# A message-passing kernel on one core: the general path moves from the else-side of a branch to a branch of its own

## The chip, the core and the metric

The kernel runs on one core of one Trainium2 chip. The core has a matrix engine (PE, with its weight loads shown as PEld), a vector engine (DVE), an activation engine (ACT), a general engine (POOL) and a queue engine (SP) that issues transfers. Each of them has its own stream of instructions, takes its own branches, and meets the others only through semaphores: an instruction may wait until a semaphore has reached a number, and may add to one when it is done. The metric is the device time of one execution in microseconds; smaller is better. Times of before and after are medians of several runs.

## What is computed

The reference takes 1250 nodes with 512 features each and 40000 edges sorted by their target, and makes one block of an equivariant network (PaiNN), adds its input, and normalizes each row:

```python
x_j = x[src]
s_j = silu(x_j[:, 384:] @ W1 + b1) @ W3 + b3
edge_basis = rbf * cutoff @ W2 + b2
s1, s2, s3 = split(s_j * edge_basis)
v_msg = v_j * s1[:, :, None] + s3[:, :, None] * edge_attr1[:, None, :]
x = x + segment_sum(concatenate([v_msg, s2]), dst)      # first sum over edges
...
msg = update(x[src])                                     # U, V, Wu1, Wu2
x = x + segment_sum(msg, dst)                            # second sum over edges
return layernorm(x_in + x)
```

## The kernel before

A front part loads nodes, edges and weights, turns the node features into a table of 640 numbers per node in memory (`table1`, L584), and counts how many chunks of 512 edges have a target outside of the window of nodes that the fast path keeps for them (`missed_i`, L290). L383 loads that count into a register on every engine, and L384 branches on it: with a count of zero the engines run `windowed` (L587), otherwise `general` (L528), which is good for any order of edges. With the inputs of the reference the count is zero, so `general` is in the program but never runs. Before the change it is the else-side of the same branch (L386).

`windowed` goes over 79 steps. A step is four tiles of 128 edges (512 edges, of four chunks). In the order of the code (L1490 to L1503) step t does this:

- DVE makes the messages of the step (`messages`, L860): `hot` (L812) compares the edges' targets with the lanes, then L865, `pair` (L883), `spread` (L823) and L869 multiply the gathered rows with the edge factors `eb`. All of it reads `eb`, which has one buffer, and `hot` is the first that waits for it.
- PE adds up the messages of the step before (`add_messages`, L893: L900 four matmuls, L907 twelve), counts links (`count_links`, L914: L925 four), and then makes the next step's factors (`edge_factors`, L850: L854 four matmuls). These last cannot start before DVE's L869 has read the old factors. PE has some work besides in most steps (node updates), and from step 32 on it also begins the large second product (`begin_out`, L1257; `products`, L1245: the matmuls of L1248).
- POOL issues the four gathers for three steps later (`gather`, L739; L745), the first of them behind PE's `edge_factors`.
- ACT prepares one-hot tiles (L835, L845) and copies.

The program's extra work repeats every eight steps, so steps that lie eight apart do the same things. The next step's `hot` waits for PE's L854, and L854 waits for DVE's L869: this circle sets the pace. After the steps come the rest of the second product, the normalization and the output (`end_out` L1276, `norm_out` L1289, stores at L1303).

The build handles semaphores as follows. Each engine has one counting semaphore, and a waiting instruction waits for a number of it. The build takes an increment away where nobody waits for its number and adds it to a later increment of the same engine. Numbers run through the whole program. With the two paths as two sides of one branch, both start from the same number and must end at the same number; the shorter side gets its missing counts from one large increment at its start. Read out of the built program: PE stands at 42 when the branch comes; `windowed` counts from 42 to 2446; `general` starts with one increment of 1076 and counts from 1118 to 2446. On DVE it is `windowed` that starts with a large increment (1618), and on ACT too (324). Transfer semaphores are filled up in the same way: SP has eight semaphore instructions and POOL eight instructions (INC_SWDGE_SEM, reported under L1873) in `windowed` that do nothing else. An increment stays when a waiting instruction of either path names its number. So PE's matmuls of `windowed` mostly lose their increments below 1118 and mostly keep them above:

| matmuls of PE with an increment, built program before | steps 1 to 37 | steps 38 to 66 | steps 67 to 70 | steps 71 to 75 |
|---|---|---|---|---|
| of how many in a step | 24 to 32 | 26 to 34 | 31 to 34 | 26 to 34 |
| that increment | 1 to 4 | 18 in step 38, then 26 to 34 | 13 to 17 | 20 to 34 |

Of the kernel before, what the change touches and what calls it, by code (L numbers as in the profile page):

```python
# [64 lines left out]
def gnn_resnorm(  # L65
# [315 lines left out]
    front_scope.close()  # L381

    misses_v = nc.values_load(missed_i[0:1, 0:1], min_val=0, max_val=n_edges)  # L383
    with tc.If(misses_v == 0) as in_windows:  # L384
        windowed(tc, sh)
    with in_windows.Else():  # L386
        general(tc, sh)


# [1138 lines left out]
def general(tc, sh):  # L1528

    with ExitStack() as ctx:
        _general(ctx, tc, sh)
# [338 lines left out]
```

## Time and profile before

| | |
|---|---|
| median of 3 runs (lowest to highest) | 594.64 us (591.26 to 596.64) |
| the profiled execution's own time | 585.79 us |
| its span, first to last instruction | 583.8 us |
| mean granted clock of PE | 0.888 |
| busy PE / DVE / ACT / POOL | 445.5 / 441.8 / 373.6 / 354.5 us |
| all 16 transfer engines, mean over the span | 217 GB/s |
| the branch L384: PE, ACT, SP, DVE take it at | 25.7, 28.0, 28.7, 30.7 us |
| first and last `hot` (L812) | 41.0 and 537.7 us |
| end of `windowed`: SP leaves it at | 579.4 us |

A row of the timeline has start, duration, engine, line, operation, output and inputs, and in brackets how long the engine was idle before it and what ended that. A row of the windows view has the stretch, its length, each engine's busy time with its number of instructions, PE's granted clock, the transfer engines' busy share and GB/s. A row of the view of one source line has the queue, the operation, its number, shortest/median/longest duration in ns, and the first and last start. A 32-bit matmul leaves two rows in the trace, so a group of four matmuls reads "x8" and the twelve of L907 read "x24".

### The profile page before, as it was taken

The page shows a single profiled execution, that of the slowest core. Times are in us where ns is not written, and L with a number is a line of the kernel's source. Part 1 is how long each engine was busy: PE and PEld are TensorE (multiplying, and loading weights), DVE is VectorE, ACT ScalarE, POOL GpSimd, SP SyncE. Part 2 cuts the span into 40 slices and gives each one's busy share as a digit, 9 for nine tenths or more (in the row PEclk, how much of TensorE's full clock was granted, in tenths as well). Part 3 has the DMA queues.
Part 4 walks back from the last instruction along what each step waited for, and adds up shares of the span by engine and source line. Part 5 has one row for each costly group of instructions (what it writes and reads, how often), then busy time and mean ns, then how long its engine had stood idle before and what let it go on. Part 6 is the DMA issues. An engine that isn't in the chain of part 4 may idle for free. (4 is left out here: it accounts for less than half of the span.)

```text
span 583.8 us, 11028 instructions
## 1 busy us (share of the span) xinstructions
PE 445.5 (76%) x4193; PEld 240.2 (41%) x4193; DVE 441.8 (76%) x698; ACT 373.6 (64%) x941; POOL 354.5 (61%) x369
## 2 busy tenths in 40 slices
PE   2845667687777887697888786787777878798894
PEld 1422323344444344334435443443443444353673
DVE  7685867878878777878877777777787777687685
ACT  1455364757677665767776767777667778656455
POOL 7265767656667665656656665666666576643850
PEclk9966986888899777979888889998989899889998
DMA  8766777786777767767877777777777787859514
GB/s 240 257 189 213 200 224 216 210 262 200 216 224 243 228 197 218 214 205 220 253 245 201 253 226 213 233 231 242 220 229 224 218 240 224 241 148 285 210 38 146
DMA packets 38321, 126.95 MB, mean 217 GB/s; under 512 B 6688, under 2 KB 8238, under 8 KB 38258
## 3 DMA queue, kind: packets, MB, share of 16 engines
q0 software_dynamic: 26016, 104.86, 60.5%
q1 hardware_dynamic: 10910, 20.64, 10.2%
q10 hardware_dynamic: 1332, 0.64, 0.4%
q8 instruction: 35, 0.57, 0.4%
q14 instruction: 28, 0.23, 0.1%
HBM read 114.78 MB, written 11.34 MB: 216 GB/s over the span
## 5 line engine op out<-in xcount | busy, mean ns | idle before, releaser
L745 POOL DMA_INDIRECT more<-table,src_i x189 | 189.9, 1005 | 107.3 <-issue 44.0
L745 POOL DMA_INDIRECT nodes<-table,src_i x124 | 126.3, 1019 | 74.0 <-issue 28.3
L854 PE MATMUL eb<-w_sb,basis_t 25*128 25x388 f32 x626 | 83.5, 585 | 76.6 <-issue 42.2
L845 ACT ACTIVATE one<-one,weight,src_f 128x128 f16<-128x128 f16 x313 | 128.5, 482 | 0.5 <-issue 0.2
L835 ACT ACTIVATE one<-number,low 128x128 f16<-128x128 f16 x313 | 99.8, 392 | 8.5 <-PE adj L925 3.3
L812 DVE TENSOR_TENSOR hot<-lane,eb 128x128 f32<-128x128 f32 (+1 forms) x81 | 22.7, 281 | 81.6 <-PE eb L854 44.7
L869 DVE TENSOR_TENSOR more<-more,eb 128x1536 f32<-128x1536 f32 (+2 forms) x49 | 82.6, 1688 | 0.0
L854 PEld LDWEIGHTS eb<-w_sb,basis_t 25*128 25x128 f32 x626 | 27.5, 196 | 99.5 <-issue 58.0
L900 PE MATMUL agg<-more,hot 128*32 128x512 f32 (+1 forms) x378 | 66.0, 752 | 1.2 <-ACT sums L956 1.2
L865 DVE TENSOR_TENSOR more<-more,eb 128x1024 f32<-128x1024 f32 (+2 forms) x49 | 57.5, 1175 | 0.4 <-issue 0.3
L907 PEld LDWEIGHTS agg<-more,spread 128*32 128x32 f32 x1134 | 39.5, 125 | 40.8 <-issue 40.1
L869 DVE TENSOR_TENSOR nodes<-nodes,eb 128x1536 f32<-128x1536 f32 (+1 forms) x32 | 54.2, 1695 | 0.0
L907 PE MATMUL agg<-more,spread 128*32 128x128 f32 x1134 | 47.8, 298 | 0.0
L823 DVE TENSOR_TENSOR spread<-hot,eb 128x384 f32<-128x384 f32 (+1 forms) x81 | 43.0, 532 | 0.0
L925 PE MATMUL adj<-pair,one 128*128 128x160 f16 x313 | 37.9, 243 | 5.0 <-issue 4.9
L900 PE MATMUL agg<-nodes,hot 128*32 128x512 f32 x248 | 38.5, 680 | 2.4 <-ACT sums L956 2.4
L883 DVE TENSOR_TENSOR pair<-number,column 128x640 f16<-128x640 f16 (+1 forms) x81 | 38.5, 476 | 0.0
L805 ACT COPY basis_t<-work 128x512 f32<-128x512 f32 x20 | 11.7, 587 | 41.1 <-PE work L800 21.7
L865 DVE TENSOR_TENSOR nodes<-nodes,eb 128x1024 f32<-128x1024 f32 (+1 forms) x32 | 37.8, 1180 | 0.0
L960 DVE SCALAR_TENSOR_TENSOR both<-both,adj 128x400 f16<-128x400 f16 (+1 forms) x20 | 11.3, 566 | 32.0 <-ACT both L951 21.1
L907 PEld LDWEIGHTS agg<-nodes,spread 128*32 128x32 f32 x744 | 23.6, 116 | 23.1 <-issue 22.9
L925 PEld LDWEIGHTS <-one 128*128 128x128 f16 x313 | 20.8, 100 | 22.1 <-issue 20.7
(258 smaller groups left out, 728.8 us busy)
## 6 DMA issues: line engine op xcount, KB each, us to landing
table<-more SPq DMA_DIRECT2D x10, 320.0 KB
spilled<-begun SPq DMA_DIRECT2D x12, 256.0 KB
more<-table,src_i POOLq DMA_INDIRECT x189
more<-spilled SPq DMA_DIRECT2D x2, 1280.0 KB
resid<-h_t SPq DMA_DIRECT2D x9, 256.0 KB
node_x<-in_x_dram SPq DMA_DIRECT2D x8, 256.0 KB
nodes<-table,src_i POOLq DMA_INDIRECT x124
nodes<-in_x_dram POOLq DMA_DIRECT2D x2, 768.0 KB
```

Source lines behind the costliest of these rows:

```text
L745: got = nc.gpsimd.indirect_dma_start(out=rows_t[:n, j, :], out_offset=None, in_=sh.table1, in_offset=bass.IndirectOffsetOnAxis(ap=sh.src_i ...
L812: nc.vector.tensor_tensor(hots[t][:m, js, :], lane[:m, None, :WIN].to_broadcast(shape), eb[:m, js, V + 3 : V + 4].to_broadcast(shape), op= ...
L823: nc.vector.tensor_mul(spread[t][:m, js], hots[t][:m, js, None, :].to_broadcast(shape), eb[:m, js, V : V + 3, None].to_broadcast(shape),)
L835: nc.scalar.activation(onehots[t][:, j, :], number[:, :P], AF.Abs, bias=low[:, e : e + 1])
L845: nc.scalar.activation(one, one, AF.Relu, scale=less[:, e : e + 1], bias=worth[:, e : e + 1])
L854: made = nc.tensor.matmul(eb[:, j, : V + CARRY], turned[g][rows, i, :], sh.w2_sb[rows, :], start=True, stop=True,)
L865: nc.vector.tensor_mul(msg[:m, js, V:], msg[:m, js, V:], eb[:m, js, C:V])
L869: nc.vector.tensor_mul(msg[:m, js, :V].rearrange("p t (k c) -> p t k c", k=3), msg[:m, js, :V].rearrange("p t (k c) -> p t k c", k=3), eb[ ...
L883: nc.vector.tensor_tensor(pair[:m, js, :].rearrange("p t (l h) -> p t l h", h=2), number[:m, : PARTS * WIN].rearrange("p (l h) -> p l h", ...
L900: nc.tensor.matmul(agg[j * WIN : (j + 1) * WIN, :], hots[t][:m, j, :], msg[:m, j, :width], start=(i == 0), stop=False, skip_group_check=True,)
L907: nc.tensor.matmul(agg[j * WIN : (j + 1) * WIN, c * C : (c + 1) * C], spread[t][:m, j, c, :], msg[:m, j, width:], start=False, stop=(i == ...
L925: nc.tensor.matmul(to[:, :, at : at + WIN], one[:m, j, :], pair[:m, j, :].rearrange("e (p n) -> e p n", n=WIN), start=(i == 0 and j == js[ ...
```

## The change

The condition is tested twice instead of once. `general` gets a branch of its own, behind the one of `windowed`, with the opposite condition on the same register:

```diff
     misses_v = nc.values_load(missed_i[0:1, 0:1], min_val=0, max_val=n_edges)
-    with tc.If(misses_v == 0) as in_windows:
+    with tc.If(misses_v == 0):
         windowed(tc, sh)
-    with in_windows.Else():
+    with tc.If(misses_v != 0):
         general(tc, sh)
```

No line of `windowed`, and no line of what comes before it, differs. What the build makes of it differs. The two paths now follow each other in the program and in the semaphores' numbers: PE counts in `windowed` from 42 to 2446 and in `general` from 2446 on; DVE's and ACT's large increments at the start of `windowed` are gone. The order of the engines' instructions in `windowed` is the same, except for these:

| in `windowed` of the built program | before | after |
|---|---|---|
| PE matmuls with an increment, of 2404 | 1359 | 276 |
| of these in a step, steps 38 to 75 | 13 to 34 | 2 to 5 |
| DVE instructions with an increment, of 646 | 636 | 363 |
| ACT, of 903 | 827 | 772 |
| SP's semaphore instructions that fill up a count | 8 | 0 |
| POOL's INC_SWDGE_SEM | 8 | 0 |

The number for which an instruction waits stands for the same releasing instruction as before. Each branch without an else gets a small block that fills up the counts when the branch is not taken: eight semaphore instructions and a jump on SP, a semaphore instruction, four waits, one INC_SWDGE_SEM and a jump on POOL, a semaphore instruction and a jump on each of the others. With these inputs every engine leaves `windowed` by a jump over the first such block, tests the condition again (L386), jumps over `general` to the second such block, runs it, and goes on to the end of the program. Before, it jumped over `general` straight to the end. In SP's stream the first of the two jumps goes over 9 instructions, the jump over `general` over some 430.

## The prediction

> **What bounds the kernel now.** I read the page first, then the timeline around single steps, then windows cut at the starts of steps, and the rows of the branch and of the end last. No engine is full:
>
> ```profile
> span 583.8 us, 11028 instructions
> PE 445.5 (76%) x4193; PEld 240.2 (41%) x4193; DVE 441.8 (76%) x698; ACT 373.6 (64%) x941; POOL 354.5 (61%) x369
> ```
>
> PE and DVE are both busy for 76% and wait for each other in each of the 79 steps: DVE's `hot` (L812) needs PE's factors (L854), and L854 needs DVE's L869. The row of L812 shows where these steps lie, 496.7 us from the first `hot` to the last:
>
> ```profile
> L812 DVE TENSOR_TENSOR hot<-lane,eb x81: 172/286/289, 41.0 to 537.7; 128x128 f32<-128x128 f32 x76, 128x64 f32<-128x64 f32 x4, 64x32 f32<-64x32 f32 x1
> ```
>  So the pace of a step decides, and of it the hole between DVE's L869 and the next `hot`.
>
> The built program offers a comparison inside this one trace. Up to step 37 a step's matmuls carry 1 to 4 semaphore increments; from step 38 to 66 nearly every one of the 26 to 34 carries one. The change makes the second kind of step into the first. So I cut two stretches of 32 steps each, steps 7 to 38 and 39 to 70, each four rounds of the eight-step pattern, and two single rounds out of the first:
>
> ```profile
> 87.60:287.30 199.70, 155.54 (x1593) 82.52 (x1586) 155.76 (x225) 132.89 (x340) 129.92 (x128) 0.85 0.74 222
> 287.30:492.10 204.80, 165.69 (x1692) 87.70 (x1695) 156.71 (x228) 147.53 (x370) 129.09 (x128) 0.93 0.76 229
> ...
> 185.80:237.60 51.80, 40.92 (x410) 22.26 (x402) 39.22 (x57) 34.98 (x89) 32.18 (x32) 0.80 0.71 213
> 237.60:287.30 49.70, 38.84 (x403) 19.86 (x396) 39.45 (x58) 33.77 (x88) 32.52 (x32) 0.86 0.75 224
> ```
>
> The first column after the stretch is its length. The stretch with many increments takes 204.80 us against 199.70, that is 6.40 against 6.24 us a step, although PE's granted clock was higher in it (0.93 against 0.85). DVE's busy time is the same (156.71 and 155.76): the difference is waiting.
>
> Now the hole itself, in steps of equal place in the pattern. The first four pairs have few increments, the last four many; each pair is L869 and the next step's `hot`:
>
> ```profile
> 103.36 1.75 DVE L869 TENSOR_TENSOR nodes<-nodes,eb 128x1536 f32<-128x1536 f32 x1
> ...
> 106.17 0.29 DVE L812 TENSOR_TENSOR hot<-lane,eb 128x128 f32<-128x128 f32 x1 [0.29 <-PE eb L854]
> ...
> 201.72 1.74 DVE L869 TENSOR_TENSOR more<-more,eb 128x1536 f32<-128x1536 f32 x1
> ...
> 204.63 0.28 DVE L812 TENSOR_TENSOR hot<-lane,eb 128x128 f32<-128x128 f32 x1
> ...
> 233.75 1.75 DVE L869 TENSOR_TENSOR more<-more,eb 128x1536 f32<-128x1536 f32 x1
> ...
> 237.61 0.29 DVE L812 TENSOR_TENSOR hot<-lane,eb 128x128 f32<-128x128 f32 x1 [1.71 <-PE work L1103]
> ...
> 265.00 1.75 DVE L869 TENSOR_TENSOR more<-more,eb 128x1536 f32<-128x1536 f32 x1
> ...
> 268.94 0.29 DVE L812 TENSOR_TENSOR hot<-lane,eb 128x128 f32<-128x128 f32 x1 [1.60 <-PE eb L854]
> ```
>
> ```profile
> 406.14 1.74 DVE L869 TENSOR_TENSOR more<-more,eb 128x1536 f32<-128x1536 f32 x1
> ...
> 409.48 0.29 DVE L812 TENSOR_TENSOR hot<-lane,eb 128x128 f32<-128x128 f32 x1 [0.36 <-PE begun L1248]
> ...
> 457.10 1.75 DVE L869 TENSOR_TENSOR more<-more,eb 128x1536 f32<-128x1536 f32 x1
> ...
> 460.50 0.29 DVE L812 TENSOR_TENSOR hot<-lane,eb 128x128 f32<-128x128 f32 x1 [0.41 <-PE begun L1248]
> ...
> 334.62 1.75 DVE L869 TENSOR_TENSOR more<-more,eb 128x1536 f32<-128x1536 f32 x1
> ...
> 338.76 0.29 DVE L812 TENSOR_TENSOR hot<-lane,eb 128x128 f32<-128x128 f32 x1 [1.99 <-PE begun L1248]
> ...
> 418.11 1.75 DVE L869 TENSOR_TENSOR nodes<-nodes,eb 128x1536 f32<-128x1536 f32 x1
> ...
> 422.35 0.29 DVE L812 TENSOR_TENSOR hot<-lane,eb 128x128 f32<-128x128 f32 x1 [1.89 <-PE begun L1248]
> ```
>
> From L869's start to `hot`'s start: 2.81 and 2.91 us with few increments against 3.34 and 3.40 (same place, +0.51); 3.86 against 4.14 (+0.28); 3.94 against 4.24 (+0.30). The brackets change too: with many increments `hot` starts so late that the view names L1248, which PE runs behind L854. No view lists increments one by one; in the trace's record of them, sixteen of PE's come right ahead of the `hot` at 409.48, one each 0.040 us, the last 0.024 us before it. They come out in single file, and the one that `hot` waits for is the last in the file.
>
> **The change, part by part.** (a) PE's increments. Of steps 38 to 75, 38 steps, about nine in ten increments go. The gain of a step has two ends. The two stretches give 0.16 us (5.10 over 32). Without the round at clock 0.80, which is the slowest of the first stretch, its other 24 steps took 147.90 us, 6.16 each, and the gain is 0.24. I take 0.20, between them, and not the 0.36 that the pairs give on average, because the stretches hold all places of the pattern, those too in which `hot` waits for something else. 38 times 0.20 is 7.6 us; ends 6.1 and 9.1. Behind step 75, matmuls are large: the increments of L1248 are there further apart than 0.040 us, and I count nothing. What is late next in a step is L854 itself, and beneath that POOL's four gathers (32.18 to 32.52 us busy of a round of about 50), so the circle stays the bound.
>
> (b) DVE's 273 and ACT's 55 increments: nothing. DVE's work from `hot` to the end of L869 is bounded by DVE's rows above, L869 takes 1.74 to 1.75 us in both stretches, and its busy times agree within 0.95 us over 32 steps.
>
> (c) POOL's eight INC_SWDGE_SEM and SP's eight semaphore instructions at the start of `windowed`:
>
> ```profile
> L1873 POOLq INC_SWDGE_SEM  x8: 328/354/405, 31.5 to 38.8; - x8
> L1873 SPq EVENT_SEMAPHORE  x3: 17/17/17, 28.8 to 32.9; - x3
> ...
> 36.92 0.94 POOL L745 DMA_INDIRECT more<-table,src_i  x1 [0.30 <-issue]
> 38.17 1.15 POOL L745 DMA_INDIRECT more<-table,src_i  x1 [0.30 <-issue]
> ...
> 47.20 0.95 POOL L745 DMA_INDIRECT more<-table,src_i  x1 [0.30 <-issue]
> 48.45 0.95 POOL L745 DMA_INDIRECT nodes<-table,src_i  x1 [0.30 <-issue]
> ```
>
> A gather follows the one before it by 1.25 us with such an instruction between them (36.92 to 38.17) and without (47.20 to 48.45): it runs beside the gather. The cover is DVE, which is busy until its first `hot` at 41.0. Nothing; without that cover up to eight times 0.354, 2.8 us, would be gained.
>
> (d) The end. SP is the last to leave:
>
> ```profile
> 578.59 0.74 SPq L1303 DMA_DIRECT2D out_dram<-h_t  x2
> ...
> L384 SPq COMPARE_BRANCH  x2: 46/48/49, 28.7 to 579.4; - x2
> ...
> L1873 SPq EVENT_SEMAPHORE  x14: 17/28/28, 582.1 to 583.7; - x14
> ```
>
> It jumps over `general` at 579.4, and its next instruction starts at 582.1: 2.7 us for a long jump. At the start of the kernel the branch into the next instruction took 0.1 us (28.7 to 28.8). The change adds a jump over 9 instructions, a test, eight semaphore instructions and a jump to the next block, and keeps one long jump. The 14 rows from 582.1 to 583.7 bound a semaphore instruction by 0.12 us; I take 0.07 since barrier waits are among them, so 0.6 for eight, and 0.1 for each of two short jumps: +0.8. The upper bound takes the short jump over 9 instructions as dear as the long one: +3.5. The last transfer, issued by 579.3, is hidden behind the long jump and stays so.
>
> [...] No row here shows a short taken jump.
>
> The sum, against the profiled execution's own 585.8 us: −7.6 + 0.8 = −6.8, so 579.0. The median of the runs shown is 8.8 us above that execution; I carry the difference over: 594.6 − 6.8 = 587.8 us.
>
> **The rivals.** First: increments cost nothing on the path, and the second stretch is slower because it has the begun products, L1248. For it: those matmuls belong to the second stretch nearly alone:
>
> ```profile
> 237.60:287.30 49.70, 1.44 (x4) 0.60 (x4) 0.86 0.75 224
> 287.30:338.80 51.50, 8.39 (x22) 3.57 (x22) 0.90 0.76 231
> ```
>
> Against it: in most steps they stand behind L854 in PE's order, where they cannot hold up its own `hot`, and the hole has grown there as well; and the file of increments ends at `hot`. Then only the end counts: 595.4 us. Chance 0.20.
>
> Second, on the other side: the jump over 9 instructions fetches anew like the long one. Place: SP's way to the end, where nothing covers it; price 2.7 us more, 3.5 together. It decides the sign where the steps give less than 3.5 us, that is less than 0.09 us each. With no gain the time is 598.1. Chance 0.07, as both must hold.
>
> Third: the pairs' 0.36 us is true of all steps: 38 times 0.36 less 0.8 is 12.9, and 581.7 us. Against it speaks the difference of the stretches. Chance 0.11.
>
> Fourth: each increment taken away shortens its step by its whole 0.040 us. Some 27 a step in 38 steps are 41 us, and 554 us. The pairs' 0.28 to 0.51 instead of 1.1 speak against it. Chance 0.02. [...]
>
> **How the numbers follow.** My forecast, that the steps give 4 to 10 us, has a chance of 0.60. It runs from 585 to 591 us alone. Within 1%, about what a measurement of this kernel can tell from no change, is 588.7 to 600.6. In three quarters of the forecast (0.18 us or more a step) the time is under that: 0.45, and with the third and fourth rival 0.58. Over it lie only cases in which the end costs still more: 0.03. Within: 0.39. The range that should hold the time 8 times in 10 runs from the third rival nearly to the first: 582.0 to 595.5.
>
> **What would show it.** Right: 32 steps from step 39 on take about 198.5 us instead of 204.80; the hole in the places of 409.48 and 460.50 is 2.9 us or less; `hot` there is released by PE's L854. At the end one more branch row (L386) on each engine, no INC_SWDGE_SEM around 31 us, and about 0.8 us more between SP's last store and the last instruction. Wrong: the second stretch keeps its 6.40 us a step with its increments gone (first rival); 5 us between SP's branch and its next instruction (second); or PE's granted clock in that stretch falls from 0.93 to 0.80, where the round at 185.80 took 51.80 us, and takes the gain back.

## The result and the profile after

| | before | after |
|---|---|---|
| median of 20 runs (lowest to highest) | 592.17 us (588.34 to 598.86) | 589.95 us (584.46 to 595.90) |
| ratio | | 0.9943, 95% interval 0.9922 to 0.9963 |
| profiled execution: own time, span | 585.79, 583.8 us | 584.46, 582.6 us |

By the ratio the kernel became faster by 3.4 us (2.2 to 4.6), half of the 6.8 us of the forecast, and within 1%. The ratio is taken over undisturbed runs alone; the medians, over all runs, differ by 2.2 us. The time of 589.95 us lies in the range, 2.2 us above the 587.8 of the forecast. That it lies so near is in part luck: the forecast started from a median of three runs, 594.64 us, and that of the 20 is 2.5 us lower; from the latter the forecast would have been 585.4, 4.6 us too low. Of the cases, the one that had 0.58, faster by more than 1%, did not come.

The increments are gone as foreseen. Here are after's stretches, cut at the same steps (start of step 7, 39, 71 and 76), and the last of these stretches in before:

```profile
87.06:287.93 200.87, 155.62 (x1602) 82.74 (x1598) 155.93 (x224) 133.31 (x340) 129.69 (x128) 0.86 0.75 221
287.93:490.62 202.69, 163.63 (x1677) 86.85 (x1670) 156.90 (x229) 147.20 (x369) 128.92 (x128) 0.92 0.77 233
490.62:519.69 29.07, 24.95 (x262) 12.57 (x266) 23.63 (x37) 20.73 (x56) 16.89 (x17) 0.94 0.70 204
```

```profile
492.10:522.81 30.71, 25.45 (x256) 12.37 (x252) 23.72 (x36) 21.23 (x56) 16.77 (x17) 0.89 0.69 199
```

Steps 39 to 70 took 202.69 us instead of 204.80 (198.5 were forecast), steps 71 to 75 29.07 instead of 30.71: together 3.75 us less over 37 steps, 0.10 a step. The first stretch, in which PE's increments did not change, took 1.17 us more (200.87 against 199.70). So one pair of executions tells such stretches apart to no better than about 1 us. In the experiments it is worse: there the 37 steps took 188.1 to 191.1 us in the six kernels that have few increments in all steps and no added work.

The hole between L869 and the next `hot` shrank in the places shown in the prediction. In the timeline of after, the same four steps of the second half:

```profile
405.09 1.75 DVE L869 TENSOR_TENSOR more<-more,eb 128x1536 f32<-128x1536 f32 x1
...
408.00 0.29 DVE L812 TENSOR_TENSOR hot<-lane,eb 128x128 f32<-128x128 f32 x1
...
455.77 1.75 DVE L869 TENSOR_TENSOR more<-more,eb 128x1536 f32<-128x1536 f32 x1
...
458.85 0.29 DVE L812 TENSOR_TENSOR hot<-lane,eb 128x128 f32<-128x128 f32 x1
...
334.25 1.75 DVE L869 TENSOR_TENSOR more<-more,eb 128x1536 f32<-128x1536 f32 x1
...
338.20 0.29 DVE L812 TENSOR_TENSOR hot<-lane,eb 128x128 f32<-128x128 f32 x1 [1.80 <-PE begun L1248]
...
416.35 1.75 DVE L869 TENSOR_TENSOR nodes<-nodes,eb 128x1536 f32<-128x1536 f32 x1
...
420.35 0.29 DVE L812 TENSOR_TENSOR hot<-lane,eb 128x128 f32<-128x128 f32 x1 [1.64 <-PE eb L854]
```

From start to start 2.91, 3.08, 3.95 and 4.00 us, against 3.34, 3.40, 4.14 and 4.24 before: 0.43, 0.32, 0.19 and 0.24 less. The prediction had set 2.9 us or less for the first two, and `hot` released by L854; the second misses the first of these, and the view still names L1248 at the third.

The end grew more than foreseen. The rows of SP's stores, its two branches and its semaphore instructions in after (queue, number, shortest/median/longest duration in ns, first and last start):

```profile
575.37 0.74 SPq L1303 DMA_DIRECT2D out_dram<-h_t  x2
...
L384 SPq COMPARE_BRANCH  x2: 44/45/46, 27.8 to 576.2; - x2
...
L386 SPq EVENT_SEMAPHORE  x8: 17/17/17, 578.9 to 579.4; - x8
L386 SPq COMPARE_BRANCH  x1: 50/50/50, 576.3 to 576.3; - x1
...
L1873 SPq EVENT_SEMAPHORE  x14: 17/28/28, 579.5 to 582.6; - x14
```

The jump over 9 instructions took 0.19 us (576.157 to 576.344 in the trace's record), the eight semaphore instructions 0.6 us, the long jump 2.5 us (2.7 in before). But the 14 instructions of the end take 3.1 us (579.5 to 582.6) where before had 1.6 (582.1 to 583.7): between the second and the third of them SP stands still for 1.54 us. From the start of the last store to the end it is 6.90 us instead of 4.78: 2.1 us more, not 0.8.

Step by step against before, at the start of step 39 after stood 0.6 us later, at step 76 3.1 us earlier, at the last store 3.2 earlier, at the end 1.1 earlier.

### The profile page after: what moved, and what is told of

It is laid out like the page before. It is cut to its first block, busy times and chain, and to the rows that moved or that the text cites. A ratio compares the mean times of both kernels' runs of the same rounds, so it can differ in the third digit from the quotient of the medians.

```text
span 582.6 us, 11033 instructions
## 1 busy us (share of the span) xinstructions
PE 444.0 (76%) x4193; PEld 240.9 (41%) x4193; DVE 441.8 (76%) x698; ACT 373.5 (64%) x941; POOL 355.1 (61%) x369
## 5 line engine op out<-in xcount | busy, mean ns | idle before, releaser
L745 POOL DMA_INDIRECT more<-table,src_i x189 | 191.1, 1011 | 102.1 <-issue 45.2
L854 PE MATMUL eb<-w_sb,basis_t 25*128 25x388 f32 x626 | 83.7, 583 | 77.0 <-DVE more L869 35.1
L869 DVE TENSOR_TENSOR more<-more,eb 128x1536 f32<-128x1536 f32 (+2 forms) x49 | 82.7, 1690 | 0.0
L854 PEld LDWEIGHTS eb<-w_sb,basis_t 25*128 25x128 f32 x626 | 28.7, 198 | 99.3 <-DVE more L869 42.9
L900 PE MATMUL agg<-more,hot 128*32 128x512 f32 (+1 forms) x378 | 62.0, 708 | 0.5 <-ACT sums L956 0.4
L865 DVE TENSOR_TENSOR more<-more,eb 128x1024 f32<-128x1024 f32 (+2 forms) x49 | 57.6, 1176 | 0.2 <-issue 0.2
L869 DVE TENSOR_TENSOR nodes<-nodes,eb 128x1536 f32<-128x1536 f32 (+1 forms) x32 | 54.3, 1698 | 0.0
L900 PE MATMUL agg<-nodes,hot 128*32 128x512 f32 x248 | 40.8, 715 | 1.5 <-ACT sums L956 1.5
L865 DVE TENSOR_TENSOR nodes<-nodes,eb 128x1024 f32<-128x1024 f32 (+1 forms) x32 | 37.8, 1182 | 0.0
L907 PEld LDWEIGHTS agg<-nodes,spread 128*32 128x32 f32 x744 | 26.0, 123 | 24.4 <-issue 23.9
L907 PE MATMUL agg<-nodes,spread 128*32 128x128 f32 x744 | 30.7, 297 | 0.0
```

What stands on the lines that cost most here:

```text
L745: got = nc.gpsimd.indirect_dma_start(out=rows_t[:n, j, :], out_offset=None, in_=sh.table1, in_offset=bass.IndirectOffsetOnAxis(ap=sh.src_i ...
L854: made = nc.tensor.matmul(eb[:, j, : V + CARRY], turned[g][rows, i, :], sh.w2_sb[rows, :], start=True, stop=True,)
L865: nc.vector.tensor_mul(msg[:m, js, V:], msg[:m, js, V:], eb[:m, js, C:V])
L869: nc.vector.tensor_mul(msg[:m, js, :V].rearrange("p t (k c) -> p t k c", k=3), msg[:m, js, :V].rearrange("p t (k c) -> p t k c", k=3), eb[ ...
L900: nc.tensor.matmul(agg[j * WIN : (j + 1) * WIN, :], hots[t][:m, j, :], msg[:m, j, :width], start=(i == 0), stop=False, skip_group_check=True,)
L907: nc.tensor.matmul(agg[j * WIN : (j + 1) * WIN, c * C : (c + 1) * C], spread[t][:m, j, c, :], msg[:m, j, width:], start=False, stop=(i == ...
```

## The experiments

The theory: PE's increments come out one behind the other (0.040 us apart ahead of the `hot` at 409.48 in the result's trace of before), the last is the one `hot` waits for, and a step with many of them loses some 0.1 us; the end gives 2.1 us back. Rivals: the increments cost nothing and the second half is slow by its products (L1248); or it is DVE's and ACT's increments that cost, which went at the same time.

The three groups of experiments ran on three chips. There the kernel before takes 499 to 500 us instead of the 592 of the runs of the result, at a mean granted clock of about 0.95 instead of 0.888. The last section says what differs. Ratios are to the kernel before on the same chip. In every kernel the order of the instructions in `windowed` is that of before, unless said.

**One branch, `general` twice in its else-side** (increments of PE dense, that is on most matmuls, from step 1 on), on two chips:

```diff
     with in_windows.Else():
-        general(tc, sh)
+        general(tc, sh), general(tc, sh)
```

> The branch of before with its else-side holding the general path twice. The else-side never runs; but the build now keeps an increment on 9 to 32 of the matmuls of nearly every step from 1 to 37 as well (PE matmuls with an increment 1359 to 2228 of 2404). DVE's, ACT's and POOL's streams keep their increments and their order, and steps 38 to 78 are as before. So this doubles the suspected cost, in steps that have no begun products (L1248), and leaves the rest. Theory (PE's increments come out one behind the other and hold up the hot of the next step): as the trace of after gained 3.8 us in the 37 steps 39 to 75 (0.10 us a step), 37 steps lose 3.8 us here, and between 3 and 7.4 (0.20 a step): +3.8 us against before, ratio 1.006; the stretch of the 32 steps 7 to 38 takes 203 us instead of 199.70. First rival (increments cost nothing on the path, the slow second half is slow by its begun products): 0 us, that stretch stays at 199 to 201 us. Second rival (the cost is that of DVE's and ACT's increments, which went with PE's): 0 us too.

> Once more the branch of before with the general path twice in its else-side, which never runs: increments of PE dense from step 1 on. Theory: steps 4 to 38 have the median distance from L869's end to hot that before has in steps 39 to 66, 0.07 us more where the matrix engine keeps up (2.6 us in all, ratio 1.005) and 0.16 where it lags (5.9 us, ratio 1.010). Rival (increments cost nothing): 0 us, ratio 1.000.

Measured: 1.0045 (1.0000 to 1.0089) and 1.0031 (0.9992 to 1.0070). The 1.006 and 1.005 expected lie in these intervals, but so does 1 in the second, and the first touches it; the traces decide. On the second of the chips before and after ran beside it:

> The kernel before once more, for a trace of it on the chip of this group and for how far the same kernel differs from itself: ratio 1.000 within 0.4%. On a chip where the matrix engine keeps up, the hot of a step starts 1.06 us after the end of the L869 before it in steps 4 to 38 and 1.13 us in steps 39 to 66 (medians); on a chip where it lags, 2.1 and 2.4 us. If the increments are not the cause of this difference, there is none.

> The kernel after once more, on the chip of this group. Theory: in steps 39 to 75 hot starts as early as in steps 4 to 38. Where the matrix engine keeps up that is 1.06 instead of 1.13 us behind L869, 0.07 us a step and 2.6 us over 37 steps; the end gives 2.1 us back, so 0.5 us less than before, ratio 0.999. Where it lags, 0.16 us a step by the medians, 5.9 us, less 2.1: 3.8 us less, ratio 0.9935. Rival (increments cost nothing on the path): 2.1 us more than before, ratio 1.004.

Measured: before against itself 0.9999 (0.9957 to 1.0040), after 0.9973 (0.9929 to 1.0016), which holds the 0.999 expected and not the rival's 1.004. Step 16, which has no products, in the timelines of the dense kernel and of after:

```profile
119.50 1.75 DVE L869 TENSOR_TENSOR more<-more,eb 128x1536 f32<-128x1536 f32 x1
...
121.31 0.93 PE L854 MATMUL eb<-w_sb,basis_t 25*128 25x388 f32 x8 [1.48 <-DVE more L869]
...
122.39 0.29 DVE L812 TENSOR_TENSOR hot<-lane,eb 128x128 f32<-128x128 f32 x1
```

```profile
120.86 1.75 DVE L869 TENSOR_TENSOR more<-more,eb 128x1536 f32<-128x1536 f32 x1
...
122.66 0.93 PE L854 MATMUL eb<-w_sb,basis_t 25*128 25x388 f32 x8 [1.40 <-DVE more L869]
...
123.66 0.29 DVE L812 TENSOR_TENSOR hot<-lane,eb 128x128 f32<-128x128 f32 x1
```

And step 56, which has them, in before and after:

```profile
329.48 1.75 DVE L869 TENSOR_TENSOR more<-more,eb 128x1536 f32<-128x1536 f32 x1
...
331.29 0.93 PE L854 MATMUL eb<-w_sb,basis_t 25*128 25x388 f32 x8 [0.49 <-DVE more L869]
...
332.36 0.29 DVE L812 TENSOR_TENSOR hot<-lane,eb 128x128 f32<-128x128 f32 x1
```

```profile
328.79 1.75 DVE L869 TENSOR_TENSOR more<-more,eb 128x1536 f32<-128x1536 f32 x1
...
330.59 0.93 PE L854 MATMUL eb<-w_sb,basis_t 25*128 25x388 f32 x8 [0.42 <-DVE more L869]
...
331.59 0.29 DVE L812 TENSOR_TENSOR hot<-lane,eb 128x128 f32<-128x128 f32 x1
```

L854 starts in all four 0.05 to 0.06 us behind the end of L869; `hot` follows 1.08 and 1.07 us later with many increments, 1.00 and 1.00 with few. Steps 4 to 66 look like this. The median distance from L869's end to `hot`, worked out from such pairs, in us:

| | steps 4 to 38 | steps 39 to 66 | steps 67 to 75 |
|---|---|---|---|
| before (increments few, then many) | 1.057 | 1.134 | 1.109 |
| after (few, few) | 1.056 | 1.057 | 1.057 |
| `general` twice (many, many), two chips | 1.133, 1.133 | 1.133, 1.134 | 1.108, 1.109 |

It follows the increments of PE, 0.077 us a step up to step 66, with and without L1248. In before DVE and ACT keep nearly all their increments, in after fewer (363 instead of 636, and 772 instead of 827), and in steps 4 to 38 1.057 is 1.056: they cost nothing. Both rivals fall. The record of increments shows where the 0.077 comes from: in step 56 of before L854's four matmuls leave theirs at 332.213, 332.255, 332.298 and 332.340, and `hot` starts at 332.36; in after there is one, at 331.566, and `hot` starts at 331.59. So here the file is that of L854's own four. In steps 67 to 71 L854 keeps only two or three. Step 71 of before on that chip has two, and `hot` comes 1.03 us behind L854's start:

```profile
409.49 0.93 PE L854 MATMUL eb<-w_sb,basis_t 25*128 25x388 f32 x8 [1.10 <-DVE more L869]
...
410.52 0.29 DVE L812 TENSOR_TENSOR hot<-lane,eb 128x128 f32<-128x128 f32 x1 [0.84 <-PE eb L854]
```

Sorted by L854's own increments (those that come 0.90 to 1.08 us after its start), over steps 4 to 75 of the nine traces of the experiments without added work, the median from L854's start to `hot` is as follows. In 18 of the 648 steps none comes in that time; they are left out.

| increments of L854 | 1 | 2 | 3 | 4 |
|---|---|---|---|---|
| steps | 454 | 12 | 21 | 143 |
| L854's start to `hot`, us | 1.002 | 1.028 | 1.054 | 1.079 |

By this table each increment more costs 0.026 us (0.077 for three, 1.079 against 1.002), though the four of step 56 stand 0.042 us apart. By the rows the 37 steps from 39 to 75 then lose 2.7 us: 28 times 0.077, and 0.5 in the other nine.

**The same branches with a short second path** (and with none):

```diff
     with in_windows.Else():
-        general(tc, sh)
+        first_table(tc, sh)
```

```diff
     with tc.If(misses_v != 0):
-        general(tc, sh)
+        first_table(tc, sh)
```

```diff
-    with tc.If(misses_v == 0) as in_windows:
-        windowed(tc, sh)
-    with in_windows.Else():
-        general(tc, sh)
+    windowed(tc, sh)
```

> The branch of before, but its else-side holds only the first table (some 46 instructions on PE, 29 on SP) instead of the general path, which is left out; with these inputs the else-side never runs. One branch and one jump at the end as before, with increments as sparse as in after in all steps. Theory (steps give 3.8 us, and the end of after takes 2 us of it back): 3.8 us less by the steps, and the jump at the end, now over 29 instructions of SP, takes 0.2 us instead of 2.7: 6.3 us less than before, ratio 0.989. Rival (increments cost nothing on the path): only the jump is saved, 2.5 us, ratio 0.996. If a short jump fetches too, each is 2.5 us smaller.

> After's two branches, but the second holds only the first table instead of the general path, which is left out; with these inputs it never runs. Increments as sparse as in after. At the end the two branch tests and the eight filling semaphore instructions of SP stay, the long jump goes. Theory (after gained 3.8 us in its steps and paid 2.1 at its end, of it 0.2 for the short jump, 0.6 for eight semaphore instructions, 1.5 for a second fetch): two short jumps and 0.6 us, with no fetch: 1.7 us less than before at the end, 3.8 in the steps, so 5.5 us less than before, ratio 0.991, and 0.8 more than the one-branch kernel with the short else-side. Rival (increments cost nothing): 1.7 us less than before, ratio 0.997.

> Without any branch: the general path and both tests are left out, the windowed path follows the front part directly. Increments as sparse as in after. Theory: 3.8 us from the steps, 2.8 us from the jump and the test at the end, nothing at the start, where the first hot waits for other work: 6.6 us less than before, ratio 0.989. Rival (increments cost nothing): 2.8 us less, ratio 0.995.

Measured: 0.9967 (0.9934 to 0.9999), 0.9937 (0.9899 to 0.9975), 0.9936 (0.9903 to 0.9969). From the start of the last store to the end it is 2.92, 3.67 and 2.92 us, against 4.80 in before on such a chip. In the first of the three SP's jump over 29 instructions takes 0.19 us:

```profile
L1873 SPq EVENT_SEMAPHORE  x14: 17/28/28, 489.8 to 492.0; - x14
L384 SPq COMPARE_BRANCH  x2: 46/48/49, 27.7 to 489.6; - x2
```

So the 2.5 to 2.7 us belong to the long jump over some 430 instructions alone. The trace's record of transfers fits that: here no instruction fetch starts after 474.2 us, long before the jump at 489.6, while in the result's trace of before four (8192 bytes each) start between 580.3 and 582.7, behind the long jump at 579.4.

Steps (2.7 us) and end together give 4.6, 3.8 and 4.6 us less, ratios 0.991, 0.992 and 0.991. The second and third lie in their intervals. The first does not: 1.6 us less (0 to 3.3) instead of 4.6, which is not explained. Of the recorded expectations (0.989, 0.991 and 0.989, with 3.8 us for the steps) only the second lies in its interval, and by these times alone the rival, 0.996, 0.997 and 0.995, would stand in all three. The steps' rows decide against it.

**After, with SP's part of `general` longer by 18 instructions:**

```diff
     with tc.If(misses_v != 0):
-        general(tc, sh)
+        first_table(tc, sh), general(tc, sh)
```

> After, with the first table made twice in the general path's branch, which never runs: SP's part of that branch grows by 18 instructions, and the block that is jumped to and the end of the program move back by as much in SP's stream. The increments in the windowed path are as sparse as in after. In after SP stands still a second time, 1.5 us, between the second and the third instruction of the end block, at the same place on two chips. [...] Rival (SP waits there for another engine's semaphore): the stall stays at its instruction, 6.9 us.

Measured: 0.9989 (0.9946 to 1.0032), too wide to tell 1.5 us. The rows tell it:

```profile
L1873 SPq EVENT_SEMAPHORE  x14: 17/28/28, 490.9 to 492.5; - x14
L386 SPq EVENT_SEMAPHORE  x8: 17/17/17, 490.3 to 490.9; - x8
L386 SPq COMPARE_BRANCH  x1: 50/50/50, 487.8 to 487.8; - x1
```

The 14 instructions take 1.6 us again, and from the last store to the end it is 5.39 us, not the rival's 6.9: the stall is gone, with the same semaphores waited for. So it belongs to the place of the instructions (1.54 us in after, none with 18 instructions more ahead of it). That it is a second fetch just behind the first, as the expectation for two branches with a short second path has it, was the author's estimate. In the result's trace of after an instruction fetch starts at 579.48, 0.10 us before SP stands still, and takes 0.53 us; but the padded kernel has one at the same place (490.90) without a stall, and the record does not tell whose fetch it is. So that it is a fetch is not shown.

**The two branches in the other order**, `general`'s first:

```diff
-    with tc.If(misses_v == 0):
-        windowed(tc, sh)
     with tc.If(misses_v != 0):
         general(tc, sh)
+    with tc.If(misses_v == 0):
+        windowed(tc, sh)
```

> Two branches as in after, but the general path's comes first: all engines jump over it at the start, and at the end only over a block of 9 instructions on SP. Increments as sparse as in after; two loads of function tables are added on ACT at the start. Theory: the steps give 2.6 us (0.07 each) or 5.9 (0.16), the end 2.5 (a jump of 0.2 us instead of 2.7); the start takes 2.7 us back, since DVE takes the branch at 30.7 us and is busy from there to its first hot at 41.0, which moves to 43.5 or so. So 2.4 us less than before, ratio 0.995, or 5.7 and 0.990. If the jump at the start is covered by other work, 5.1 us less, ratio 0.990, or 8.4 and 0.986. Rival (increments cost nothing): 0.2 us more, ratio 1.000.

Measured: 1.0023 (0.9984 to 1.0061). The end is 1.1 us shorter (3.69 instead of 4.80), but the first `hot` comes 6.2 us later, at 46.5 instead of 40.2:

```profile
L384 DVEq COMPARE_BRANCH  x1: 72/72/72, 29.1 to 29.1; - x1
...
L384 DVEq EVENT_SEMAPHORE  x1: 21/21/21, 33.3 to 33.3; - x1
```

DVE's jump took 4.2 us there, and PE's branch instruction lasts 4.7 us (24.1 to 28.8). DVE's next work, L681, then waits until 36.4 for a copy of ACT (L304), which stands behind a load of a function table (1.28 us) and waited for PE before that. So little covers a long jump at the start here. With the steps' 2.7 us the sum is 2.4 us more, 1.005, in the interval. The recorded theory, 0.995 or less, missed: it had 2.7 us for the start.

**More work for PE:** L900's four matmuls are made a second time in each step.

```diff
+            for j in js:
+                m = lanes(g, i, j)
+                nc.tensor.matmul(
+                    agg[j * WIN : (j + 1) * WIN, :], hots[t][:m, j, :],
+                    msg[:m, j, :width], start=False, stop=False, skip_group_check=True,
+                )
             for c in range(3):
```

> Before with more work for the matrix engine: the four matmuls of L900 are made twice in each step, so that the sums over the edges are changed (that part counts twice). About 1.0 us a step more for PE, which is busy for 4.1 of some 5.2 us on a chip where it keeps up. It is the base for the two that follow: increments are dense from step 43 on. If PE lags with it, as in the trace of the result, hot starts 1.5 to 2.5 us behind the end of L869 instead of 1.06 and 1.13, and a step takes 5.4 to 6.3 us; if PE still keeps up, the times are those of before, ratio 1.00 to 1.02.

> After with the same added work (the four matmuls of L900 twice, sums changed). Sparse increments in all steps; against the loaded kernel before they go in 33 steps, 43 to 75. Theory with a cost that does not hang on PE's load: 0.08 us a step, 2.6 us less, 2.1 us more at the end, so 0.5 us less than the loaded kernel before. Theory with a cost that grows where PE lags: 0.15 us a step, 5.0 less 2.1, so 2.9 us less. Rival (increments cost nothing): 2.1 us more.

> The loaded kernel (the four matmuls of L900 twice, sums changed) with the general path twice in the else-side, which never runs: 12 to 36 increments in each step from 1 on. Against the loaded kernel before, some 42 steps get them. Theory: 0.08 us a step, 3.4 us more; if the cost grows where PE lags, 0.15 a step, 6.3 us more. Rival: 0 us.

Measured: 1.0297 (1.0235 to 1.0359), 1.0337 (1.0278 to 1.0396), 1.0296 (1.0239 to 1.0353); medians 515.33, 516.97 and 514.68 us. Against the loaded kernel before, after's branches are 1.6 us slower now by the medians, and the dense kernel is not (0.6 us faster); with six runs each, such differences are known to about 2 us. Step 48 in the loaded kernels before and after, with the stretch of 32 steps from step 39 in each:

```profile
292.65 1.75 DVE L869 TENSOR_TENSOR more<-more,eb 128x1536 f32<-128x1536 f32 x1
...
294.74 0.93 PE L854 MATMUL eb<-w_sb,basis_t 25*128 25x388 f32 x8
...
295.82 0.29 DVE L812 TENSOR_TENSOR hot<-lane,eb 128x128 f32<-128x128 f32 x1 [0.30 <-PE work L1122]
...
246.49:421.54 175.05, 174.28 (x1939) 89.62 (x1940) 157.13 (x228) 145.41 (x368) 129.09 (x128) 1.00 0.86 267
```

```profile
293.51 1.75 DVE L869 TENSOR_TENSOR more<-more,eb 128x1536 f32<-128x1536 f32 x1
...
295.68 0.93 PE L854 MATMUL eb<-w_sb,basis_t 25*128 25x388 f32 x8
...
296.68 0.29 DVE L812 TENSOR_TENSOR hot<-lane,eb 128x128 f32<-128x128 f32 x1 [0.30 <-PE eb L854]
...
247.42:422.31 174.89, 174.34 (x1939) 89.57 (x1940) 157.22 (x228) 145.30 (x368) 128.73 (x128) 1.00 0.86 268
```

`hot` still comes 0.08 us earlier behind L854 (1.00 against 1.08), but PE is busy for 174.3 of 175 us, so L854 starts 0.08 later behind L869 (2.17 against 2.09), and L869 to `hot` is 3.17 us in both. From step 67 to step 75 each takes 5.49 us in all three loaded kernels. What is left is the end, 7.00 us instead of 4.80. With PE full here, its increments cost nothing, and the change makes the kernel slower by its end.

Steps 4 to 38 are another case. PE is not full there (167 of 185 us in the loaded kernel before), and in the dense kernel L869's end to `hot` is longer by the same 0.078 us (1.134 against 1.056). Yet that kernel as a whole is not the 3.4 us slower that were expected. The rows of DVE in these steps, in the loaded kernel before and in the dense one, show where the time may have gone (behind the second bar stands DVE's idle time ahead of the line, and what ended it):

```profile
L865 DVE TENSOR_TENSOR more<-more,eb 128x1024 f32<-128x1024 f32 x21 | 25.5, 1214 | 4.0 <-DMA more<-table,src_i 4.0
L865 DVE TENSOR_TENSOR nodes<-nodes,eb 128x1024 f32<-128x1024 f32 x15 | 18.2, 1215 | 1.5 <-DMA nodes<-table,src_i 1.5
L812 DVE TENSOR_TENSOR hot<-lane,eb 128x128 f32<-128x128 f32 x36 | 10.3, 285 | 9.2 <-PE eb L854 9.0
```

```profile
L865 DVE TENSOR_TENSOR more<-more,eb 128x1024 f32<-128x1024 f32 x21 | 25.5, 1215 | 2.7 <-DMA more<-table,src_i 2.4 <-issue 0.3
L865 DVE TENSOR_TENSOR nodes<-nodes,eb 128x1024 f32<-128x1024 f32 x14 | 17.0, 1214 | 0.5 <-DMA nodes<-table,src_i 0.5
L812 DVE TENSOR_TENSOR hot<-lane,eb 128x128 f32<-128x128 f32 x36 | 10.3, 286 | 11.6 <-PE eb L854 11.2
```

`hot` waits 2.4 us longer for L854, and L865 2.3 us less for its gathers. So a later `hot` can be taken back by the gathers, which come no later for it. This rests on one trace of each, and such waits differ by 1 to 3 us between traces, so it is not shown. Neither of the two sizes of the expectation set against each other came: the load did not make PE lag as in the result's trace, it made PE the bound, from step 43 on.

## Why the prediction was half right

- **That the increments delay `hot`, and the gain's sign:** right, and shown step by step, in steps without products too. The first rival had 0.20 and was wrong.
- **0.20 us a step (the term of 7.6 us):** too large. The trace of after gives 0.10 (3.75 us over 37 steps). The 20 runs give 3.4 us, and with the end's 2.1 us 5.5 (4.3 to 6.7) for the steps, 0.15 each (0.12 to 0.18); by the medians over all runs (2.2 us) it is 0.12. In the experiments it is 0.077 where PE keeps up, and zero where PE is full (3.17 us from L869 to `hot` in both loaded kernels). The times of the eight runs without added work and with another program than before leave 1.9 us for the steps on average (-0.2 to 4.0), when their ends and starts are taken by their rows, where the rows give 2.7. Both ends of my bracket, 0.16 and 0.24, came from comparing stretches with different work in one execution; the repeat moved such a stretch by 1.17 us, and leaving out the slowest round only moved the middle up.
- **The fourth rival:** I counted every increment of a step, 0.040 us each, and it gave 41 us. In the experiments only those of the four matmuls that `hot` waits for count, 0.026 us each: 2.7 us by their rows.
- **DVE's and ACT's increments, POOL's eight instructions: nothing.** Right for the first by the table of medians. For POOL: on one chip the first `hot` comes at 40.2 us in before and in after.
- **The end, +0.8 us:** failed. 0.2 for short jumps and 0.6 for eight instructions are right, the short jump takes 0.19 us and not the long one's 2.5 (second rival, 0.07, wrong), but the 1.5 us of a second stall were not in the sum. The forecast's two terms (7.6 less 0.8) are 5.1 us more than the same two in the trace (3.75 less 2.1): 3.8 of it are the steps, 1.3 the end.
- **PE's clock** stayed at 0.92 in the second stretch; it took nothing back. The cases of 12.9 us and of 41 us did not come.

What stays open: how the cost of a step in the result's traces splits. In before's, sixteen increments stood in a file ahead of the `hot` at 409.48, in the experiments' step 56 four; no experiment ran as slowly as the result's runs. Where `hot` comes 1.9 to 2.6 us behind L854's start there, the median of steps 39 to 75 is 2.29 us in before and 2.20 in after; but in steps 4 to 38, where PE's increments did not change, it is 2.08 and 2.16, so the 0.10 between the first two tells little.

## What to carry to other kernels

Count the increments of the few matmuls that the next engine waits for (0.026 us each here), not those of the whole step, and ask first if PE has slack: the same change shortened the wait by 0.077 us a step, or gained nothing, with PE's load. A block of code that never runs is not free: it decides which increments the other path keeps, and how far the last engine must jump with nothing to cover it (0.19 us over 9 or 29 instructions, 2.5 to 2.7 us over some 430). Price such an end by its own rows on SP, since here it took back two fifths of the gain (2.1 of 5.5 us).

## What the runs showed of the hardware besides

In the runs of the result the chip is slower in a way that the mean clock does not tell. There L854 starts as promptly behind L869, but `hot` follows late. In before, this step has few increments:

```profile
233.75 1.75 DVE L869 TENSOR_TENSOR more<-more,eb 128x1536 f32<-128x1536 f32 x1
...
235.55 0.93 PE L854 MATMUL eb<-w_sb,basis_t 25*128 25x388 f32 x8 [0.80 <-issue]
...
237.61 0.29 DVE L812 TENSOR_TENSOR hot<-lane,eb 128x128 f32<-128x128 f32 x1 [1.71 <-PE work L1103]
```

`hot` comes 2.06 us after L854's start instead of 1.00, although the modelled duration is 0.93 in both. It comes more than 1.5 us after it in 58 of the 72 steps 4 to 75 of before and in 55 of after, and in two and four steps of the same kernels on the second chip of the experiments. The granted clock changes between full and half 53 times in the result's trace of before and 19 times in before's trace on that chip. Twice the time for the same matmuls would be half the clock in these steps. But the record of the clock has full clock in the step shown, from 230.6 to 247.6 us, so the cause is not settled.
